# TensorE's order from block 26 to 103 of a graph layer: made block by block instead of pair by pair

## The chip, the cores and the metric

The kernel runs on one core of one Trainium2 chip. The metric is the device time of one execution in microseconds. The core's engines work from queues of their own and meet through semaphores: TensorE (PE: matrix products; PEld: its weight loads), VectorE (DVE), ScalarE (ACT), GpSimd (POOL) and SyncE (SP). Here GpSimd only issues gathers, and SP the other transfers.

## The reference, cut to what matters

One graph layer with a residual connection and a layer norm over 8192 nodes of 256 features and 131072 edges, which are sorted by their target node:

```python
ea = edge_attr @ w_e + b_e                       # [131072, 64] x [64, 256]
msg = relu(x[src] + ea)
agg = segment_sum(msg, dst, 8192)
t = x + agg
h_local = bn1(relu(t @ w1 + b1) @ w2 + b2 + x)
# attention among the 32 nodes of each group, 4 heads of 64
h_attn = bn2(attention(x) @ out_w.T + out_b + x)
out = h_local + h_attn
out = bn3(out + relu(out @ m_w1 + m_b1) @ m_w2 + m_b2)
result = layernorm(x + out)
```

## The kernel before, in words

**Edge work** goes in 128 blocks of 1024 edges. For block b:

- `gather(b)` (L152) fetches the rows x[src] with eight indirect DMAs that GpSimd issues (L157), into `xs`, a tile with four buffers. The first 20 blocks (NX) read x; the later ones read `xb`, a copy of x + b_e that the kernel itself makes in DRAM. `copy_load` (L612) loads a part of x, `copy_stream` (L617) adds b_e on VectorE (L621) and writes the part out (L623).
- `edge_products(b)` (L195) multiplies the transposed edge attributes by w_e (L208) into `pe`, two buffers of two PSUM banks. For the first 20 blocks it also adds b_e by a product (L203).
- `edge_messages(b)` (L219) adds `xs` on VectorE (L229, two halves for each block) and takes the relu on ScalarE (L233). The `xs` buffer is free after the additions.
- `next_edges(b)` (L213) transposes the edge attributes of a later block on VectorE (L190) and loads those of one two further on.
- `edge_hot(b)` (L236) builds one-hot matrices on VectorE (L241).
- `edge_sums(blocks)` (L248) sums the messages of one or two blocks by products with the one-hot matrices (L255) into the PSUM tile `pw`; ScalarE copies it to `ws` (L265), and VectorE builds a second one-hot matrix (L269).
- `edge_place(...)` (L272) puts the sums at their nodes by a product (L280) into `l2`, which shares its one PSUM bank with `pw`; VectorE adds them to the node tile `xT` (L289).

**Node work** goes in 16 chunks of 512 nodes: `attention_front` (L424: transposes, query and key products at L445), `attention_back` (L452: values at L459, scores at L476, softmax, attention at L514, output at L526) and `dense` (L535: four layers at L545, transposes at L582, layer norm, store at L598). `dense` of a chunk may start when the last block that reaches it is placed. The last two chunks are cut into five parts.

**The order.** TensorE's queue is in the order in which the code is written (`tc.manual_schedule(engines={PE})`, L700); until block 26 (NV) VectorE's and ScalarE's are too, and from then on a scheduler orders these two. The node work lies in four streams of generators. `work.run(us)` (L651) lets them emit so many microseconds, by the planner's own costs (1.7 for a step of four matrix rows of 512); what is over or under is carried on in `owed`, to 2.0 at most. A generator that yields REST or PAUSE is left out for two or one calls of `run` (L654, L664). So the number of `run` calls counts, beside their sum. PER = 5.1 us and PER_X = 4.2 us (for the first 20 blocks) are a block's share of node work.

Until TAIL = 104 the loop at L739 goes by pairs of blocks: both gathers, the first block's products and messages, the sums of the former pair, the second block's products and messages, the placing, node work in between. Below NV the shares of a pair's node work are 0.3, 0.2 and 0.5; from NV on 0.2, 0.1, 0.2 and 0.5. From TAIL on a planner (L781 to L827) orders by times: gathers arrive every 10.035 us (`came`), and the step that is due goes next. `s` and `l` are the next block to be summed and to be placed.

Of the kernel before, what the change touches and what calls it, by code (L numbers as in the profile page):

```python
# [40 lines left out]
NV = 26  # L41
TAIL = 104
# [18 lines left out]
def first_node(b):  # L61
    return b * NPB - SLACK[b]
# [10 lines left out]
def gnn_kernel(ctx: ExitStack, tc: tile.TileContext, x, src, dst, edge_attr, w, out):  # L73
# [72 lines left out]
    def bank2():  # L146
        return pps.tile([P, 2, CH], FP, name="pe", tag="pe", bufs=2)
# [4 lines left out]
    def gather(b):  # L152
        xs = epool.tile([P, NH, TJ, C], FP, name="xs", tag="xs", bufs=4)
        for h in range(NH):
            for j in range(TJ):
                idx = srcd[:, b * NH + h, j : j + 1] if b < ND else srci[:, b, h * TJ + j : h * TJ + j + 1]
                nc.gpsimd.indirect_dma_start(  # L157
                    out=xs[:, h, j, :],
                    out_offset=None,
                    in_=x if b < NX else xb[:, :],  # L160
                    in_offset=bass.IndirectOffsetOnAxis(ap=idx, axis=0),
                )
        xs_of[b] = xs
# [31 lines left out]
    def edge_products(b):  # L195

        eaT = eaT_of.pop(b).rearrange("p (h m) r -> p h (m r)", h=NH)
        for h in range(0, NH, 2):
            pe = bank2().rearrange("p i (u c) -> p i u c", u=2)
            half = [slice(i * ED, (i + 1) * ED) for i in range(2)]  # L200
            if b < NX:
                for i, rows in enumerate(half):
                    nc.tensor.matmul(  # L203
                        pe[:, i], sel[rows, :], be[rows, None, :].to_broadcast([ED, 2, C]), start=True, stop=False, skip_group_check=True
                    )
            for u in range(2):
                for i, rows in enumerate(half):
                    nc.tensor.matmul(  # L208
                        pe[:, i, u, :], eaT[rows, h + u], we[rows, :], start=(b >= NX), stop=True, skip_group_check=True
                    )  # L210
            pe_of[b, h] = pe

    def next_edges(b):  # L213
        if b < NB:
            edge_transpose(b)
        if b + 2 < NB:
            load_edges(b + 2)
# [18 lines left out]
    def edge_hot(b):  # L236

        oh = oh_of[b] = epool.tile([P, TB, WN], FP, name="oh", tag="oh", bufs=2)
        for t0 in range(0, TB, TB // 2):
            ts = slice(t0, t0 + TB // 2)  # L240
            nc.vector.tensor_tensor(  # L241
                oh[:, ts],
                iota_n[:, None, :WN].to_broadcast([P, TB // 2, WN]),
                rel[:, b, ts, None].to_broadcast([P, TB // 2, WN]),
                ALU.is_equal,
            )
# [45 lines left out]
    stated = [True]  # L292
# [336 lines left out]
    def copy_some(n=1):  # L629
        for _ in range(n):  # L630
            next(copying[0], None)
# [63 lines left out]
    work = Work(4)  # L695
    PER = 5.1
    PER_X = 4.2
    OTHER = ("vn", "qk", "oT", "pr", "o")
    placed = -1
    with tc.manual_schedule(engines={PE}):  # L700

        def last_of(c, t_z=TN):

            return max(b for b in range(NB) if first_node(b) < c * CH + t_z * P)

        def summed(c, t_z=TN):
            last = last_of(c, t_z)
            return lambda: placed >= last and chunk[c].get("done") and not xp_of and b > 2

        for c in range(NCH):  # L710
            st, before, same = chunk[c], chunk[c - 1], chunk[c - 4]
            front = attention_front(c * CH, st, npool, bank)
            if c < 2:
                next(front)
            work.add(
                FRONT,
                lambda c=c, b=before, s=same: (c < 1 or b.get("scores"))
                and (c < 4 or s.get("dense")),
                front,
            )  # L720
            work.add(BACK, lambda s=st: s.get("front"), attention_back(st, npool, bank, bank2))
            if c < NCH - 2:
                work.add(DENSE, summed(c), dense(c * CH, st, npool, bank))
        for i, c, t_a, t_z in (
            (DENSE2, NCH - 2, 0, 2), (DENSE, NCH - 2, 2, 4), (DENSE2, NCH - 1, 0, 2), (DENSE, NCH - 1, 2, 3),
            (DENSE2, NCH - 1, 3, 4),
        ):
            d = dense(c * CH, chunk[c], npool, bank, t_a, t_z, *([OTHER] if i == DENSE2 else []))
            ready = summed(c, t_z)
            if i == DENSE2:  # L730
                ready = lambda r=ready: r() and chunk[NCH - 1].get("done")
            work.add(i, ready, d)

        spots.append(copy_some)
        early = ExitStack()
        early.enter_context(tc.manual_schedule(engines={mybir.EngineType.DVE, mybir.EngineType.Activation}))
        sums, waiting = None, []
        b = 0
        while b < TAIL:  # L739
            if b == NV:  # L740
                early.close()
                stated[0] = False
            blocks, per = range(b, b + 2), 2 * (PER_X if b < NX else PER)
            copying[0] = copy_stream(b // 2 - 1)
            for i in blocks:
                if i + 2 < NB:
                    gather(i + 2)
                if 4 <= i < 8:
                    wt, name = ((w1, "w1"), (w2, "w2"), (mw1, "m_w1"), (mw2, "m_w2"))[i - 4]
                    nc.sync.dma_start(wt, w[name].rearrange("(k p) m -> p k m", p=P))  # L750

            if b:
                edge_products(b)
                edge_messages(b)
                next_edges(b + 2)
            if waiting:
                sums = edge_sums(waiting)
            waiting = list(blocks)
            if not stated[0]:
                work.run(0.2 * per)  # L760
            edge_products(b + 1)
            edge_messages(b + 1)
            next_edges(b + 3)
            if stated[0]:
                for i in blocks:
                    edge_hot(i)
                    copy_some(2)
            work.run((0.3 if stated[0] else 0.1) * per)
            copy_load(b // 2)
            if sums:  # L770
                edge_place(*sums)
                placed, sums = sums[0][-1], None
            work.run(0.2 * per)
            if not stated[0]:
                for i in blocks:
                    edge_hot(i)
            work.run(0.5 * per)
            copy_some(4 * TN)
            b += 2

        came = [7.9 + 10.035 * (i + 1) for i in range(NB)]  # L781
        t, p, m, s, l = came[b - 2] + 20, b, b, b - 2, b - 2
        added = dict((i, came[i] + 2.0) for i in range(b))
        summed_at, bank_free = {}, t
        work.at = [t] * len(work.streams)
        while l < NB:

            times = [1e9] * 4
            if l < s:
                times[0] = summed_at[l] + 1.5  # L790
            elif s < m:
                times[1] = max(added[s] + 1.2, bank_free)
            if p < NB and m == p:
                times[2] = added[p - 1]
            if m < p:
                times[3] = came[m]
            if t >= times[0]:
                edge_place(*sums)
                placed = l
                t += 0.75  # L800
                bank_free = work.placed_at = t + 0.7
                l += 1
            elif t >= times[1]:
                sums = edge_sums([s])
                t += 1.2
                summed_at[s] = t
                s += 1
            elif t >= times[2]:
                if p + 2 < NB:
                    gather(p + 2)  # L810
                edge_products(p)
                next_edges(p + 2)
                edge_hot(p)
                t += 2.1
                p += 1
            elif t >= times[3]:

                with ExitStack() as behind:
                    for i in newest.values():
                        behind.enter_context(tc.issue_after(i))  # L820
                    edge_messages(m)
                added[m] = max(t, came[m], added[m - 1] + 0.5) + 2.0
                m += 1
            elif l == s - 1 == NB - 1:
                t = times[0]
            else:
                t = work.step(t, min(times))  # L827
        work.finish()
# [124 lines left out]
```

## Time and profile before

| | |
|---|---|
| median of 3 runs (range) | 1314.89 us (1314.71 to 1315.25) |
| the profiled execution: its time, its span | 1315.3 us, 1313.3 us |
| busy: TensorE, weight loads | 1196.5 us (91%), 720.4 us (55%) |
| busy: VectorE, ScalarE, GpSimd | 800.9 (61%), 589.2 (45%), 976.1 us (74%) |
| mean granted TensorE clock | 0.959 of full |
| DMA | 240.34 MB, 183 GB/s |

The span goes from the first to the last instruction; an execution's time holds about 2 us more. In a timeline row the columns are start, duration (us), engine, line, operation, output <- inputs and how many were merged; in brackets stand the idle time of the engine just before it and what ended it. In a table of waits they are the engine and line that waited, for whom, microseconds in total, times, and the longest.

### The profile page before, as it was taken

The page shows a single profiled execution, that of the slowest core. Times are in us where ns is not written, and L with a number is a line of the kernel's source. Part 1 is how long each engine was busy: PE and PEld are TensorE (multiplying, and loading weights), DVE is VectorE, ACT ScalarE, POOL GpSimd, SP SyncE. Part 2 cuts the span into 40 slices and gives each one's busy share as a digit, 9 for nine tenths or more (in the row PEclk, how much of TensorE's full clock was granted, in tenths as well). Part 3 has the DMA queues.
Part 4 walks back from the last instruction along what each step waited for, and adds up shares of the span by engine and source line. Part 5 has one row for each costly group of instructions (what it writes and reads, how often), then busy time and mean ns, then how long its engine had stood idle before and what let it go on. Part 6 is the DMA issues. An engine that isn't in the chain of part 4 may idle for free.

```text
span 1313.3 us, 20960 instructions
## 1 busy us (share of the span) xinstructions
PE 1196.5 (91%) x7635; PEld 720.4 (55%) x7635; DVE 800.9 (61%) x1629; ACT 589.2 (45%) x841; POOL 976.1 (74%) x1032
## 2 busy tenths in 40 slices
PE   4987989999999989898997998989898999989987
PEld 3554655556555655554554554545556555555655
DVE  5567665756666565745646574565647558475754
ACT  2524443454545363544544444353454445444433
POOL 6777777777777777777777777777777777777772
PEclk8988999999999989998998998989898999999989
DMA  9999876677766665755757566576567567655742
GB/s 234 283 338 273 263 210 175 172 183 193 177 170 170 169 183 162 195 155 157 194 157 185 154 185 168 154 186 170 170 169 189 149 169 193 162 162 161 193 129 58
DMA packets 148905, 240.34 MB, mean 183 GB/s; under 512 B 27934, under 2 KB 112188, under 8 KB 148028
## 3 DMA queue, kind: packets, MB, share of 16 engines
q0 software_dynamic: 49152, 134.28, 38.0%
q1 hardware_dynamic: 98556, 104.65, 29.5%
q8 instruction: 62, 1.02, 0.3%
q14 instruction: 47, 0.39, 0.1%
q10 hardware_dynamic: 1088, 0.00, 0.0%
HBM read 222.06 MB, written 16.78 MB: 182 GB/s over the span
## 4 chain that ended last, share of the span: by engine, by line
PE 49%; POOL 20%; issue 10%; DMA 9%; DVE 7%; ACT 4%; SPq 0%; DVEq 0%; POOLq 0%; ACTq 0%
POOL xs L157 20%; PE at L545 13%; PE pe L208 10%; PE at L445 6%; DMA xs<-xb,srci 5%; PE pw L255 5%; PE at L526 3%; PE l L280 3%; PE pe L203 2%; DVE msg L229 2%; PE at L459 2%; DMA xs<-in_x_dram,srci 2%; PE at L514 1%; ACT pr L486 1%; DVE bd L506 1%
## 5 line engine op out<-in xcount | busy, mean ns | idle before, releaser
L157 POOL DMA_INDIRECT xs<-xb,srci x864 | 820.7, 950 | 263.4 <-issue 245.1
L233 ACT ACTIVATE msg<-msg 128x1024 f32<-128x1024 f32 (+1 forms) x259 | 270.0, 1046 | 402.6 <-DVE msg L229 398.6
L229 DVE TENSOR_TENSOR msg<-pe,xs 128x1024 f32<-128x1024 f32 (+1 forms) x259 | 306.5, 1205 | 196.0 <-PE pe L208 75.8
L208 PE MATMUL pe<-we,eaT 64*128 64x256 f32 x2048 | 267.8, 398 | 17.0 <-ACT pr L486 11.8
L208 PEld LDWEIGHTS pe<-we,eaT 64*128 64x128 f32 x2048 | 193.6, 192 | 121.2 <-issue 62.7
L157 POOL DMA_INDIRECT xs<-in_x_dram,srci x144 | 138.3, 961 | 43.9 <-issue 39.9
L255 PE MATMUL pw<-msg,oh 128*32 128x256 f32 x2048 | 128.8, 384 | 1.4 <-ACT msg L233 1.0
L545 PE MATMUL at<-hA,mw 128*128 128x512 f32 (+2 forms) x304 | 124.8, 538 | 3.4 <-DVE hA L555 3.4
L445 PE MATMUL at<-xT,inT 128*128 128x512 f32 x256 | 121.9, 602 | 3.2 <-ACT xT L435 3.2
L545 PE MATMUL at<-m,mw 128*128 128x512 f32 (+2 forms) x304 | 119.0, 534 | 0.1
L190 DVE STREAM_TRANSPOSE eaT<-ea 128x512 f32<-128x512 f32 x128 | 89.9, 702 | 24.7 <-PE pe L208 20.7
L255 PEld LDWEIGHTS pw<-msg,oh 128*32 128x32 f32 x2048 | 59.5, 110 | 63.3 <-issue 22.9
L280 PEld LDWEIGHTS l<-oh,ws 128*128 128x128 f32 x512 | 74.4, 196 | 28.1 <-issue 20.9
L280 PE MATMUL l<-oh,ws 128*128 128x160 f32 (+4 forms) x512 | 86.3, 309 | 2.4 <-ACT ws L265 1.6
L545 PEld LDWEIGHTS at<-hA,mw 128*128 128x128 f32 x304 | 54.1, 192 | 51.6 <-issue 40.8
L545 PEld LDWEIGHTS at<-m,mw 128*128 128x128 f32 x304 | 54.6, 192 | 48.7 <-issue 44.9
L445 PEld LDWEIGHTS at<-xT,inT 128*128 128x128 f32 x256 | 46.9, 191 | 57.5 <-issue 48.3
L448 ACT ACTIVATE qk<-at,vec 128x512 f32<-128x512 f32 x64 | 43.9, 685 | 74.9 <-PE at L445 74.8
L545 PE MATMUL at<-xT,w 128*128 128x512 f32 (+2 forms) x152 | 68.5, 588 | 7.4 <-DVE xT L289 7.4
L545 PE MATMUL at<-h,w 128*128 128x512 f32 (+2 forms) x152 | 65.0, 550 | 9.6 <-ACT oT L521 6.3
L561 ACT ACTIVATE m<-at,vec 128x512 f32<-128x512 f32 (+2 forms) x76 | 46.8, 618 | 56.5 <-PE at L545 56.2
L570 DVE SCALAR_TENSOR_TENSOR zT<-at,s,zT 128x512 f32<-128x512 f32 (+2 forms) x38 | 25.1, 662 | 72.0 <-PE at L545 72.0
(113 smaller groups left out, 1228.3 us busy)
## 6 DMA issues: line engine op xcount, KB each, us to landing
ea<-in_edge_attr_dram SPq DMA_DIRECT2D x512, 128.0 KB
xs<-xb,srci POOLq DMA_INDIRECT x864
xn<-in_x_dram SPq DMA_DIRECT2D x16, 512.0 KB
out_dram<-y SPq DMA_DIRECT2D x14, 512.0 KB
xp<-in_x_dram SPq DMA_DIRECT2D x10, 512.0 KB
xb<-xp SPq DMA_DIRECT2D x10, 512.0 KB
xp<-in_x_dram SPq DMA_DIRECT2D x3, 1024.0 KB
xb<-xp SPq DMA_DIRECT2D x3, 1024.0 KB
```

What stands on the lines that cost most here:

```text
L157: nc.gpsimd.indirect_dma_start(out=xs[:, h, j, :], out_offset=None, in_=x if b < NX else xb[:, :], in_offset=bass.IndirectOffsetOnAxis(ap= ...
L190: nc.vector.transpose(eaT, ea[:, QR:].rearrange("p (g d) -> p g d", d=ED)[:, :, :QR])
L208: nc.tensor.matmul(pe[:, i, u, :], eaT[rows, h + u], we[rows, :], start=(b >= NX), stop=True, skip_group_check=True)
L229: nc.vector.tensor_add(msg[:, hs, js].rearrange("p u i c -> p i u c"), pe[:, js, u : u + n, :], xs[:, hs, js].rearrange("p u i c -> p i u c"),
L233: nc.scalar.activation(msg[:, hs, js], msg[:, hs, js], AF.Relu)
L255: nc.tensor.matmul(pw[h * WN : (h + 1) * WN, i, :], oh[:, h * TJ + j, :], msg[:, h, j, :], start=(j == 0), stop=(j == TJ - 1), skip_group_ ...
L280: nc.tensor.matmul(l2[:, k, at : at + wn], ws[:, i, k * P : (k + 1) * P], oh2[:, i, :wn], start=(i == 0 and k == 0), stop=(i == last), ski ...
L445: nc.tensor.matmul(ps, inT[:, k, o * P : (o + 1) * P], xT[:, k, :], start=(k == 0), stop=(k == KC - 1))
L448: nc.scalar.activation(qk[:, o, :], ps, AF.Identity, bias=v_("in_b", o))
L526: nc.tensor.matmul(ps, outT[:, k, o * P : (o + 1) * P], oT[:, k, :], start=(k == 0), stop=(k == KC - 1))
L545: nc.tensor.matmul(ps, wt[:, k, o * P : (o + 1) * P], act[:, k, :], start=(k == 0), stop=(k == nk - 1))
L561: nc.scalar.activation(m1[:, o, :], layer(mw1, KC, o, hA), AF.Relu, bias=v_("m_b1", o))
```

## The change

The pair loop ends at block 26. There the two last shares of a pair become one of 0.7, so that a pair has two calls of `run` instead of three. A new loop goes through blocks 26 to 103 one by one: the gather, products, messages, the next edges, the sums of the former block, 0.3 of a block's node work, the placing, 0.2, the one-hot matrices, 0.5. The planner then starts with one block to be summed instead of two.

```diff
-        while b < TAIL:
-            if b == NV:
-                early.close()
-                stated[0] = False
+        while b < NV:
...
             waiting = list(blocks)
-            if not stated[0]:
-                work.run(0.2 * per)
             edge_products(b + 1)
             edge_messages(b + 1)
             next_edges(b + 3)
-            if stated[0]:
-                for i in blocks:
-                    edge_hot(i)
-                    copy_some(2)
-            work.run((0.3 if stated[0] else 0.1) * per)
+            for i in blocks:
+                edge_hot(i)
+                copy_some(2)
+            work.run(0.3 * per)
             copy_load(b // 2)
             if sums:
                 edge_place(*sums)
                 placed, sums = sums[0][-1], None
-            work.run(0.2 * per)
-            if not stated[0]:
-                for i in blocks:
-                    edge_hot(i)
-            work.run(0.5 * per)
+            work.run(0.7 * per)
             copy_some(4 * TN)
             b += 2

+        early.close()
+        stated[0] = False
+        for b in range(NV, TAIL):
+            gather(b + 2)
+            edge_products(b)
+            edge_messages(b)
+            next_edges(b + 2)
+            sums = edge_sums(waiting)
+            waiting = [b]
+            work.run(0.3 * PER)
+            edge_place(*sums)
+            placed = sums[0][-1]
+            work.run(0.2 * PER)
+            edge_hot(b)
+            work.run(0.5 * PER)
+        b = TAIL
...
-        t, p, m, s, l = came[b - 2] + 20, b, b, b - 2, b - 2
+        t, p, m, s, l = came[b - 2] + 20, b, b, b - 1, b - 1
```

## The prediction

> **What bounds the kernel now.** I read the row of GpSimd's gathers first, because the busy shares at the top of the page point to the wrong engine: TensorE is busy 91% of the span, GpSimd 74%.
>
> The gather line's own view, with its number of instructions, their durations and what GpSimd waited for:
>
> ```profile
> L157 POOL DMA_INDIRECT xs<-xb,srci x864: 942/948/1072, 207.4 to 1290.2; - x173
> L157 POOL DMA_INDIRECT xs<-in_x_dram,srci x144: 942/949/1147, 25.2 to 206.2; - x144
> ```
>
> GpSimd's waits:
>
> ```profile
> POOL xs L157 <- issue: 292.2, 951, 2.6
> POOL xs L157 <- DMA xs<-xb,srci: 5.8, 19, 0.3
> POOL xs L157 <- DVE msg L229: 3.7, 12, 0.3
> ```
>
> There are 144 + 864 + 16 = 1024 gathers, the first at 4.2 us, the last from 1290.2 to 1291.2. That is 1287.0 / 1024 = 1.257 us each: 0.95 us of work and a pause of 0.30 us that is there whoever released it (the third column, the longest wait, is 0.3 even where a semaphore is named). Eight gathers make a block, so a block is delivered every 10.05 us, and GpSimd never stood still for another engine. The windows say the same at any place: 37.8 to 38.0 us of gathers in each 50 us.
>
> The second reading is how far the rest runs behind. For each block I set the end of its last message addition on VectorE (L229, two rows a block) against the start of its last gather: the distance is 31.4 us at block 14, 17.3 at block 26, 4.0 to 4.2 at blocks 51, 55, 58, 65, 75 and 83, 10.7 at 102, 12.7 at 119, and 4.2 at 124 to 126. About 4 us is the least, the flight of the gather and the two additions. The rows buffer `xs` has four copies, so gather b+4 may start only when block b's messages are added. At 31.4 us this had 0.4 us left (message end 186.9, gather 18 at 187.3); from block 26 to 103 some 14 us or more are left.
>
> The third reading is the end. First TensorE's timeline around 1260:
>
> ```profile
> 1259.42 0.70 PE L280 MATMUL l<-oh,ws 128*128 128x112 f32 x4 [0.55 <-ACT ws L265]
> 1261.73 2.08 PE L208 MATMUL pe<-we,eaT 64*128 64x256 f32 x8 [1.61 <-DVE msg L229]
> 1264.42 2.08 PE L208 MATMUL pe<-we,eaT 64*128 64x256 f32 x8 [0.61 <-DVE msg L229]
> ```
>
> At 1261.73 it waits 1.61 us for additions that wait for a gather: it has caught up and works at GpSimd's pace. Then the timeline of all engines:
>
> ```profile
> 1290.23 0.95 POOL L157 DMA_INDIRECT xs<-xb,srci  x1 [0.30 <-issue]
> ...
> 1293.00 0.42 DVE L229 TENSOR_TENSOR msg<-pe,xs 128x256 f32<-128x256 f32 x1
> ...
> 1294.50 1.09 PE L255 MATMUL pw<-msg,oh 128*32 128x256 f32 x16
> ```
>
> After the last gather a fixed chain follows: last addition until 1293.4, sums 1294.5, place 1296.4, dense layers until 1307.5, normalisation and output to 1313.3: 22.1 us.
>
> So the span is 4.2 (start) + 1287.0 (gathers) + 22.1 (chain) = 1313.3 us. The profiled execution took 1315.3 us, 2.0 more than its span; the median of the three runs shown is 1314.89, 0.4 less.
>
> **The change part by part.** *No work for GpSimd.* The same 1024 gathers stand in the same order, and only their place in the trace of the other engines moves. Cost 0, as long as each finds its buffer free.
>
> *Blocks 6 to 25.* Two shares of 0.2 and 0.5 become one of 0.7, so a pair has two visits to the node streams instead of three, and a stream that rests two visits rests longer. I counted TensorE's orders of both programs and priced them by rows (512 columns: four rows 1.88 us; products 2.00; sums of two blocks 1.93; a chunk's attention products of L514 1.97). Ahead of block 14's products stand 55 us of node work instead of 65, ahead of block 26's 114 instead of 121. The work is put off, not lost. So the point with 0.4 us left gets looser: TensorE comes up to 10 us earlier, unless the other order makes it wait. The worst such wait in this trace is 6.3 us (at L514, for VectorE's transposes of line 506), less than 10. In the same stretch the last copy of x + b_e to `xb` is issued at 195.3 us and the first gather from `xb` starts at 207.4: 12 us that also get no shorter if TensorE is earlier. I take 0; bounds 0 and, if one stall of 6.3 us fell on GpSimd in full, +6.3.
>
> *Blocks 26 to 103, instructions.* TensorE has the same 3963 matrix instructions in both orders. ScalarE has 38 more evacuations of the sums: 76 of 256 columns (0.372 us) for 38 of 512 (0.569), 28.3 - 21.6 = +6.7 us, and two more table loads of 1.28 us, +2.6. VectorE has 38 more additions at L289; from the row of 96 columns (0.239) and that of 448 (0.599) an addition's fixed part is about 0.14 us, my estimate, so +5 us, and up to 38 x 0.24 = 9. Both engines hide this: in 267 to 1060 us ScalarE is busy 373 of 793 us and VectorE 474. SP and GpSimd get nothing new. Bounds: nothing, and if each of the 38 small copies stood whole before TensorE, 38 x 0.37 = 14 us of TensorE time, within what follows.
>
> *The same blocks, TensorE's waits.* In 267 to 1060 us it is busy 737.7 of 793.0 us, so 55 us are waits, 0.70 us a block. The change removes some: a block's products now follow the former block's by some 7 us of other work always, where the pair had them 4 us apart in one place and 9.5 in the other; the largest waits named there are for messages (14.2 us at L476) and for ScalarE (10.3 us at L208). It adds one: between sums and place there was 2.0 + 0.3 x 10.2 = 5.1 us of products and node work, now 0.3 x 5.1 = 1.5 us, in practice one step of 1.72 to 1.88. The place waits for ScalarE's copy, and ScalarE has ahead of it the first half of the newer block's messages (1.07), which waits for an addition (1.22). Behind a waiting place stand the node steps and the next products; for those waits VectorE. If all three follow one another, 1.22 + 1.07 + 0.37 - 1.72 = 0.94 us a block; if the copy is free, 0. The bounds on TensorE are thus -55 us (all waits gone) and +73 us (78 x 0.94). I take 0, since the products (2.0 us) run before the sums and let addition and message pass. For the end both bounds are small: a gain of 55 us only makes TensorE wait for gathers, and a loss is first paid out of the 55.
>
> At this place a rule of the Trainium skill speaks against the change (TensorE: Matmul & The Clock Gate, "HAM oscillation"): idle gaps over some 3.4 us put the clock at half, so waits cost twice. The granted clock here is 0.90 in the window 850 to 900, which has gaps of 2.65 and 2.52 us before L476 and L545, and 1.00 in 950 to 1000, which has none over 1.2: the trace agrees in kind, but the gaps are shorter than the page's. By it, one window of 3.4 us at half clock more in each pair would be 39 x 1.7 = 66 us of TensorE time, an estimate, near the 73 above.
>
> *The handing over at 104.* The later planner starts with one block's sums open instead of two, and with less node work behind it: ahead of block 104's products 521 us instead of 528, ahead of block 103's 516 instead of 521. By block 123 both stand at the same 626.5, and TensorE's last 196 matrix instructions, from just ahead of block 123's products, stand in the same order in both, and so do VectorE's last 80. About 5 us of node work, less 1 for sums, move into blocks 104 to 123. TensorE is idle 10.7 us in 1060 to 1250 and 6.2 us in 1250 to 1291, and between the products of blocks 124 and 125 there is no node work at all, where some 3.8 of 10 us are used. So 4 to 5 us come out before the last gather. Bounds: 0, and +5 if none is absorbed.
>
> **Sum**: 1315.3 + 0 + 0 + 0 + 0 = 1315.3 on the profiled execution's scale, 1315 with the runs' 0.4 us below it. Single gathers of 1.0 to 1.15 us beside the heavy early transfers and the interleaving of 1289 to 1294 may move it by 1 to 1.5 us.
>
> **Rivals.** A measurement of this kernel tells about 0.2% (2.6 us) from no change.
>
> *TensorE falls behind (slower).* The wait at the place costs so much in each block that it exceeds the idle time. It decides from 0.70 us a block on, at block 104, and for the end from (55 + 17 - 4) / 78 = 0.87 us. At 1.2 us it is 94 + 4 - 55 - 17 = +26 us, 1341. For it: place has 1.7 us of cover, and the chain can reach 0.94. Against: it would need nearly that worst chain every time, and a TensorE that is late finds its gathers landed, so the addition starts at once. Chance 0.10.
>
> *The put-off work is late at the end (slower).* 3 to 5 us of it are still there at block 126: 1318 to 1320. For it: TensorE runs without a gap from 1274 to 1291. Against: the gaps just before. Chance 0.06. *An early stall of GpSimd*, up to +6.3, 1321: 0.04; for it the 0.4 us at block 14, against it the 10 us less work.
>
> *TensorE was the bound after all (faster).* At 91% busy, even shares would recover part of its waits, and the end would move with it. For it only the busy share; against it GpSimd's row without a wait. What can be gained is in the chain after the last gather, of which TensorE and VectorE hold some 14 us; a quarter of it would be 1311.5. Chance 0.08.
>
> *It hardly does anything to the time*: that is my forecast, 0.72. Its own range is 1313.5 to 1317.
>
> **How the numbers follow.** Slower by over 0.2%: 0.10 + 0.06 + 0.04 = 0.20. Faster: 0.08. Within: 0.72. The range takes the forecast's, the late end and the early stall, 1313 to 1321, and leaves out the falling behind and the faster case, 0.18.
>
> **What would show it.** Right: 1024 gathers from 4.2 to about 1291 with no wait over 0.3 us; message lag smaller than 31 us at block 14, at least 10 us of buffer left later; TensorE's time busy unchanged but its waits moved; a chain of 22 us after the last gather. Wrong: a GpSimd row with a wait of microseconds for L229 or for `xb`; L280 waiting for L265 by more than 55 us in all; no wait for L229 at block 125's products; a last gather that ends at 1291 and a span that is still longer.

## The result, and the profile after

The changed kernel took 1322.38 us (median of 4 runs, 1320.92 to 1324.0) against 1315.07 us (1314.71 to 1315.86) of the kernel before: a ratio of 1.0055, 95% interval 1.0038 to 1.0073. It is slower, by more than the 0.2% that counts as a difference here, and outside the forecast range of 1313 to 1321. In twelve of the eighteen runs below the kernel before itself took 1946 to 2045 us, for a reason that stays open, and nothing is concluded from their ratios.

The profiled execution took 1320.92 us with a span of 1319.1 us, 5.8 us longer than the 1313.3 us before. First GpSimd's gathers, from the gather line's own view: instructions, their least, median and longest duration in ns, first and last start.

```profile
L157 POOL DMA_INDIRECT xs<-xb,srci x864: 942/946/1186, 209.0 to 1290.5; - x173
L157 POOL DMA_INDIRECT xs<-in_x_dram,srci x144: 942/946/2112, 25.5 to 207.8; - x144
```

GpSimd's waits after:

```profile
POOL xs L157 <- issue: 295.1, 961, 2.6
POOL xs L157 <- DMA xs<-xb,srci: 3.7, 12, 0.3
...
POOL xs L157 <- DVE msg L229: 3.0, 10, 0.3
```

The last gather starts at 1290.5 us (before 1290.2), and no wait named for another engine is over 0.3 us: the gathers are as before. After the last one (it ends at 1291.4) the kernel needs 27.7 us instead of 22.1. So the time is not lost by the gathers, but by an engine that comes late to the end. TensorE's timeline after shows it (start, duration, in brackets the idle time before and what ended it):

```profile
1267.92 0.70 PE L280 MATMUL l<-oh,ws 128*128 128x112 f32 x4 [0.55 <-ACT ws L265]
1270.23 2.27 PE L208 MATMUL pe<-we,eaT 64*128 64x256 f32 x16 [1.61 <-DVE msg L229]
...
1274.04 0.70 PE L280 MATMUL l<-oh,ws 128*128 128x112 f32 x4 [0.54 <-ACT ws L265]
1275.22 2.00 PE L545 MATMUL at<-xT,w 128*128 128x256 f32 x8 [0.48 <-DVE xT L289]
...
1278.23 1.56 PE L545 MATMUL at<-h,w 128*128 128x256 f32 x6 [0.58 <-ACT h L552]
1279.72 2.00 PE L208 MATMUL pe<-we,eaT 64*128 64x256 f32 x16
...
1288.77 2.00 PE L208 MATMUL pe<-we,eaT 64*128 64x256 f32 x16
```

The products of block 127 start at 1288.77 us; before they started at 1283.52. Those of block 123 were 8.5 us late (1258.1 against 1249.6), so 3.2 us were made up between the two. The wait of 1.61 us ahead of block 125's products, which the prediction took for a wait for a gather, is there after as well, though TensorE is then 8.5 us later: it is the fixed chain from a product to its addition to the next product. The other four (0.55, 0.54, 0.48, 0.58) are there before as well, within 0.02 us. Of before's gaps in this stretch only the one of 0.61 us is gone.

Where the 5.25 us (1288.77 - 1283.52) come from is read from the windows, cut at TensorE's own events: the products of block 26, 107 and 127. Block 107 is the last of the changed kernel whose message additions end within 5 us of the start of its last gather (4.2 us; about 4 is the least): there TensorE meets the gathers for the last time. Before, it does so again at blocks 123 to 126 (4.1 to 4.9 us). Columns: from and to, length, then for PE, PEld, DVE, ACT and POOL the busy time and its instructions, the granted clock, DMA share and GB/s. Before:

```profile
0.00:290.20 290.20, 254.43 (x1647) 152.95 (x1647) 184.16 (x398) 120.92 (x173) 218.12 (x234) 0.96 0.86 239
290.20:1088.93 798.73, 741.91 (x4685) 440.31 (x4684) 481.05 (x942) 372.42 (x513) 604.83 (x637) 0.96 0.65 171
1088.93:1283.52 194.59, 179.73 (x1137) 110.19 (x1136) 122.24 (x252) 85.20 (x128) 147.34 (x156) 0.97 0.62 166
1283.52:1313.30 29.78, 20.40 (x169) 16.91 (x168) 13.48 (x39) 10.64 (x27) 5.83 (x7) 0.93 0.18 53
```

The same after:

```profile
0.00:288.47 288.47, 250.87 (x1631) 150.15 (x1632) 183.76 (x397) 118.65 (x170) 217.32 (x232) 0.95 0.85 239
288.47:1088.30 799.83, 740.88 (x4677) 433.49 (x4676) 492.64 (x974) 372.50 (x546) 605.48 (x639) 0.97 0.66 172
1088.30:1288.77 200.47, 182.44 (x1165) 112.20 (x1161) 126.07 (x259) 90.14 (x139) 151.74 (x161) 0.98 0.61 163
1288.77:1319.10 30.33, 20.41 (x169) 16.95 (x168) 12.51 (x37) 9.84 (x27) 2.02 (x3) 0.97 0.11 35
```

Up to block 107 both stand level (1088.9 and 1088.3 us), the row that holds the block-by-block stretch is 1.1 us longer, and the last row is 0.6 longer. The loss is the third row: 200.5 us instead of 194.6, with 28 more matrix instructions in it. By the order of the two programs, 98.8 us of node work stand behind block 107's products before and 104.2 after. The experiments ask whether that is the work which the merged share of 0.7 put off below block 26, carried along for 80 blocks.

### The profile page after: what moved, and what is told of

It reads as the page before. It is cut to its first block, busy times and chain, and to the rows that moved or that the text cites. A ratio compares the mean times of both kernels' runs of the same rounds, so it can differ in the third digit from the quotient of the medians.

```text
span 1319.1 us, 21143 instructions
## 1 busy us (share of the span) xinstructions
PE 1194.6 (91%) x7635; PEld 712.8 (54%) x7635; DVE 815.0 (62%) x1667; ACT 591.1 (45%) x881; POOL 976.6 (74%) x1032
## 4 chain that ended last, share of the span: by engine, by line
PE 43%; POOL 20%; DVE 12%; issue 11%; DMA 8%; ACT 5%; SPq 1%; DVEq 0%; ACTq 0%; POOLq 0%
POOL xs L157 20%; PE at L545 13%; PE pe L208 9%; PE at L445 5%; PE pw L255 4%; DVE msg L229 4%; DMA xs<-xb,srci 4%; PE l L280 3%; PE at L526 3%; PE at L459 2%; DMA xs<-in_x_dram,srci 2%; ACT msg L233 2%; PE at L514 2%; DMA ea<-in_edge_attr_dram 2%; PE pe L203 1%
## 5 line engine op out<-in xcount | busy, mean ns | idle before, releaser
L208 PE MATMUL pe<-we,eaT 64*128 64x256 f32 x2048 | 264.2, 394 | 5.1 <-ACT pr L486 3.2
L255 PE MATMUL pw<-msg,oh 128*32 128x256 f32 x2048 | 137.3, 389 | 5.7 <-DVE xT L289 5.4
L280 PEld LDWEIGHTS l<-oh,ws 128*128 128x128 f32 x512 | 76.7, 192 | 80.4 <-ACT ws L265 39.7
L280 PE MATMUL l<-oh,ws 128*128 128x160 f32 (+4 forms) x512 | 90.5, 304 | 31.5 <-ACT ws L265 25.6
L255 PEld LDWEIGHTS pw<-msg,oh 128*32 128x32 f32 x2048 | 55.9, 110 | 76.2 <-issue 37.1
L289 DVE TENSOR_TENSOR xT<-l,xT 128x320 f32<-128x320 f32 (+11 forms) x145 | 57.0, 410 | 46.0 <-PE l L280 44.8
L241 DVE TENSOR_TENSOR oh<-iota_n,rel 128x128 f32<-128x128 f32 x256 | 59.4, 272 | 21.8 <-PE pw L255 21.8
```

The source lines that it names most:

```text
L208: nc.tensor.matmul(pe[:, i, u, :], eaT[rows, h + u], we[rows, :], start=(b >= NX), stop=True, skip_group_check=True)
L241: nc.vector.tensor_tensor(oh[:, ts], iota_n[:, None, :WN].to_broadcast([P, TB // 2, WN]), rel[:, b, ts, None].to_broadcast([P, TB // 2, WN ...
L255: nc.tensor.matmul(pw[h * WN : (h + 1) * WN, i, :], oh[:, h * TJ + j, :], msg[:, h, j, :], start=(j == 0), stop=(j == TJ - 1), skip_group_ ...
L280: nc.tensor.matmul(l2[:, k, at : at + wn], ws[:, i, k * P : (k + 1) * P], oh2[:, i, :wn], start=(i == 0 and k == 0), stop=(i == last), ski ...
L289: newest["xT"] = nc.vector.tensor_add(xT, l2[:, :, a - n : z - n], xT).ins
```

## The experiments

**Theory 1** is this: the work that was put off below block 26 (6.9 us by the order) is what makes the end late, since TensorE has no free time to do it later. Against it stand theory 2, that the block-by-block order itself, with its new waits, costs the time, and theory 3, that the merged call does so in another way than by the amount put off, as by the order that it gives the chunks.

### early_back: the three calls below block 26 again, block order kept

```diff
-            work.run(0.7 * per)
+            work.run(0.2 * per)
+            work.run(0.5 * per)
```

The two calls follow each other where the changed kernel has its one, so only the count of calls differs.

> The same kernel again, since in its first runs both kernels took over 2000 us, with some 40 stretches of about 14 us in which VectorE and ScalarE stood still, which the first runs of before and after do not have. The changed kernel with the three calls (0.3, 0.2, 0.5) below block 26 restored; blocks 26 to 103 block by block. Theory 1, the end is late because node work is put off below block 26: 1314 to 1316, products of block 127 at about 1283.5 us. Theory 2, the order by blocks itself makes TensorE wait more: 1320 to 1324.

Measured: 1315.46 us (12 runs), ratio to before 1.0009 (0.9996 to 1.0022), the span of the profiled execution 1313.4. The first and third rows of its windows:

```profile
0.00:288.84 288.84, 254.72 (x1647) 153.14 (x1647) 183.77 (x398) 120.78 (x173) 217.27 (x233) 0.96 0.86 240
...
1088.82:1281.85 193.03, 176.02 (x1125) 108.42 (x1125) 119.72 (x244) 86.43 (x130) 146.06 (x154) 0.99 0.63 168
```

One line brings the time back, and the third row is 193.0 us. Ahead of block 26 TensorE is busy 254.7 us instead of 250.9 and comes to its products at the same time (288.8 and 288.5): there the work was free, and where it was left out TensorE was idle 37.6 us instead of 34.1. The block order itself costs nothing that this measurement can tell: the interval leaves at most 2.9 us.

### early_only: the merged call alone, pairs kept to block 103

```diff
-            work.run(0.2 * per)
-            if not stated[0]:
+            if stated[0]:
+                work.run(0.7 * per)
+            else:
+                work.run(0.2 * per)
                 for i in blocks:
                     edge_hot(i)
-            work.run(0.5 * per)
+                work.run(0.5 * per)
```

> The same kernel again, for the same reason. The kernel before with only the calls below block 26 changed; from 26 on pair by pair. Theory 1 (work put off, 6.9 us less node work ahead of block 104's products): 1319 to 1324. Theory 2 (the order by blocks): 1314 to 1316.

Measured: 1327.29 us (6 runs), 1.0086 (1.0068 to 1.0104), span 1325.3: later, as theory 1 says, but 3 us beyond the 1324 that was expected of it. Its third and last stage:

```profile
1085.50:1291.42 205.92, 185.43 (x1163) 115.98 (x1161) 126.25 (x259) 90.24 (x139) 154.20 (x163) 0.96 0.61 162
```

```profile
1291.42:1325.30 33.88, 24.48 (x169) 20.18 (x168) 12.52 (x37) 9.93 (x27) 0.00 (x0) 0.81 0.06 18
```

The put-off work alone makes the kernel slower than the whole change does. 104.2 us of node work are left at block 107, as in the changed kernel, and the stage takes 11.3 us more than before: 5.7 us are busy time, with 5.4 us more of work, and 5.6 are idle time. One wait of 5.3 us, put down to VectorE's normalisation (L588), is not in the changed kernel. The last stage is 4.1 us longer than before, all of it TensorE's busy time (24.5 instead of 20.4) at a granted clock of 0.81.

### pair_less: the work put off in another place, all else as before

```diff
-            blocks, per = range(b, b + 2), 2 * (PER_X if b < NX else PER)
+            blocks, per = range(b, b + 2), 2 * (PER_X if b < NX else PER if b < NV else 5.0)
```

> Pair by pair, below block 26 as before, a share of 5.0 instead of 5.1 us from 26 on: 6.9 us less node work ahead of block 104's products. Theory 1 (put-off work comes out at the end, whatever put it off): 1320 to 1328. Theory 3 (the calls below block 26 do their harm in some other way): 1314 to 1316.

Measured: 1324.78 us (8 runs), 1.006 (1.0041 to 1.0079). The profiled execution, with a span of 1328.3 us, was the longest of the eight (1321.98 to 1330.12). Calls and order are those of before; a share of 5.0 us instead of 5.1 leaves the same 104.2 us at block 107:

```profile
1088.30:1294.00 205.70, 186.56 (x1164) 116.67 (x1160) 126.17 (x259) 90.46 (x139) 153.04 (x162) 0.95 0.61 161
```

Again products of 107 at 1088.3 and a stage of 205.7 us. Work that is left late in another place comes out at the end too.

### share517 and share530: the work given back from block 26 on

```diff
-            work.run(0.3 * PER)
+            work.run(0.3 * 5.17)
```

and so for the shares of 0.2 and 0.5; share530 has 5.3. By the order, 98.8 us are left at block 107 in the first, as before, and 87.9 in the second.

> The changed kernel with a share of 5.17 instead of 5.1 us from block 26 to 103; the two calls below block 26 kept. By block 104 TensorE has had the same total as before the change (-0.1 us). Theory 1 (put-off work comes out at the end): 1314 to 1317. Theory 3 (the calls below block 26 do their harm in some other way): 1320 to 1324.

> The changed kernel with a share of 5.3 us: 12.1 us more ahead of block 104's products than before the change. If from some point on only the gathers bound the end, nothing is gained over before: 1313 to 1316. If TensorE's put-off work bounds it all along, some 10 us below before: 1303 to 1308.

Measured: share517 1320.81 us (12 runs), 1.0031 (1.0013 to 1.005), span 1317.0; share530 1330.52 us (6 runs), 1.0107 (1.0082 to 1.0131), span 1326.3. Theory 1, as it was put, missed both, the second by 14 us and more, and the first lies where theory 3 had put it (1320 to 1324). The windows of share517, blocks 26 to 107 and 107 to 127:

```profile
286.51:1093.51 807.00, 742.92 (x4718) 435.02 (x4717) 495.17 (x980) 377.33 (x556) 610.88 (x644) 0.97 0.64 171
1093.51:1286.60 193.09, 176.95 (x1124) 108.52 (x1120) 123.61 (x253) 86.09 (x129) 146.18 (x155) 0.99 0.62 165
```

And of share530:

```profile
286.50:1110.80 824.30, 761.43 (x4781) 445.42 (x4780) 503.79 (x1006) 381.37 (x565) 623.88 (x658) 0.97 0.64 171
1110.80:1295.75 184.95, 165.35 (x1059) 102.03 (x1057) 113.67 (x227) 78.83 (x118) 137.30 (x145) 0.99 0.61 161
```

The last stage answers as the theory says: 193.1 us with 98.8 left, 185.0 with 87.9. But the middle stage grew: against the changed kernel's 799.8 us by 7.2 and 24.5 us, for 5.4 and 16.3 us of work moved into it. So TensorE's idle time there (59 us) is not free time: with the work added it rose to 64 and 63 us. In share530 no message addition after block 26 ends less than 9 us behind the start of its block's last gather, where about 4 is the least: TensorE never meets the gathers any more and is itself the bound. In share517 it does meet them. Its timeline just before block 107's products:

```profile
1081.52 1.16 PE L476 MATMUL pe<-qk 64*128 64x128 f32 x16 [1.77 <-DVE msg L229]
1085.89 2.08 PE L476 MATMUL pe<-qk 64*128 64x128 f32 x16 [3.21 <-DVE msg L229]
1087.89 4.68 PE L545 MATMUL at<-m,mw 128*128 128x512 f32 x8
1092.51 1.07 PE L255 MATMUL pw<-msg,oh 128*32 128x256 f32 x16
```

And on VectorE:

```profile
1084.52 1.23 DVE L229 TENSOR_TENSOR msg<-pe,xs 128x1024 f32<-128x1024 f32 x1 [3.14 <-DMA xs<-xb,srci]
```

The scores of an attention chunk (L476) use the `pe` buffers of the products, and wait 5.0 us for additions; the second of these had itself waited 3.14 us for gathered rows. Then 4.7 us of node work come before block 107's products. Being early here is worth nothing, and TensorE reaches block 107 4.6 us later than before.

### early_more62: the work given back below block 26, calls still merged

```diff
-            blocks, per = range(b, b + 2), 2 * (PER_X if b < NX else PER)
+            blocks, per = range(b, b + 2), 2 * (PER_X if b < NX else 6.2)
```

The results so far leave two causes: the amount, or the merged call by the order that it makes. Here the order of the kernels gives 122.7 us of node work ahead of block 26 (before 120.9, changed 114.1). What is called theory 2 in the expectation is here the reading of share517, that work given back late does not land.

> The changed kernel with its share per block raised from 5.1 to 6.2 us in the pairs below block 26 that follow the first stretch; the calls stay merged there, and block order and share from 26 on stay as changed. By the order of the kernels, TensorE's node work ahead of block 26's products is 122.7 us (before 120.9, changed 114.1) and ahead of block 104's 528.1 (before 528.1, changed 521.2). Theory 1 (the amount put off past block 26 is the loss, however it is put off): products of block 127 at 1281 to 1285 us, and 1314 to 1317 us. Theory 2 (work given back later does not land, because TensorE then waits at the gathers' heels, as with the share of 5.17): here it is given back below block 26, where TensorE runs 11 us and more behind the gathers, so 1314 to 1318. Rival (the merged call itself, by the order that it gives the chunks, costs the time, and the amount is only a sign of it): 1320 to 1324, as in the changed kernel.

Measured: 1316.40 us (12 runs), 1.0007 (0.999 to 1.0024). All four stages of its profiled execution, which at 1321.27 us was one of its longer ones (1315.22 to 1323.3):

```profile
0.00:300.27 300.27, 260.00 (x1652) 152.53 (x1652) 183.95 (x397) 120.32 (x173) 225.26 (x242) 0.96 0.85 234
300.27:1090.40 790.13, 734.04 (x4691) 428.88 (x4690) 492.50 (x976) 372.97 (x551) 598.48 (x630) 0.98 0.66 173
1090.40:1284.78 194.38, 177.46 (x1129) 110.02 (x1128) 121.88 (x256) 86.88 (x130) 147.17 (x156) 0.97 0.62 165
1284.78:1319.50 34.72, 24.61 (x169) 20.11 (x168) 13.63 (x39) 10.75 (x27) 6.03 (x7) 0.80 0.16 47
```

It comes to block 26 11.8 us later than the changed kernel, for 8.6 us more work, and is at block 107 only 2.1 us behind it: the stage between is 9.7 us shorter, with 2.2 us less work, 2.9 us less idle time, and the clock at half for 37.1 us instead of 44.4. It has 97.8 us left there and needs 194.4. Block 127's products start at 1284.78, within the 1281 to 1285 expected. The calls are still merged and the time is back: the amount is the cause, and theory 3 falls. That this one execution is long lies in its last row, a clock of 0.80 and 4.2 us more of TensorE's busy time than before.

### The other runs

These are the twelve named in the first section. Share517 alone lies on both sides of before there, so they tell nothing of the theories. The double dose of put-off work, share500, thus stays untried under the conditions of the result.

Early_back: 2028.36 us, ratio 0.9971 (0.9939 to 1.0002).

> The changed kernel with one thing undone: below block 26 a pair's node work is again given out in three calls (0.3, 0.2, 0.5). Blocks 26 to 103 stay block by block. Node work ahead of block 104's products: 528.1 us, as before the change (the changed kernel 521.2). Theory 1, the end is late because about 5 us of node work are put off into blocks 104 to 123, and they were put off below block 26: back to 1314 to 1316, products of block 127 at about 1283.5 us. Theory 2, the order by blocks itself makes TensorE wait more (the placing for ScalarE's copy): stays at 1320 to 1324.

Early_only: 2029.78 us, ratio 1.0014 (0.9971 to 1.0057).

> The kernel before with only the calls below block 26 changed (0.3 and 0.7 instead of 0.3, 0.2, 0.5); from block 26 on pair by pair as before. Node work ahead of block 104's products: 521.2 us instead of 528.1. Theory 1 (work put off): 1319 to 1324. Theory 2 (the order by blocks): 1314 to 1316.

Pair_less: 2030.48 us, ratio 1.0039 (1.0007 to 1.007).

> The kernel before, pair by pair, unchanged below block 26; from 26 on a block's share of node work is 5.0 instead of 5.1 us. Node work ahead of block 104's products: 521.2 us instead of 528.1, so the same amount is put off, in another place and without any order by blocks. Theory 1 (work put off): 1319 to 1324, whatever put it off. Theory 2: 1314 to 1316.

Pair_less again: 1987.07 us, ratio 1.0106 (1.007 to 1.0143).

> Pair by pair as before, below block 26 as before, but a share of 5.0 instead of 5.1 us from 26 on: 6.9 us less node work ahead of block 104's products. Theory 1 (what is put off into blocks 104 to 123 comes out at the end, whatever put it off): 1320 to 1328. Theory 3, that the calls below block 26 do their harm in some other way than by work put off: 1314 to 1316.

Pair_less again: 1982.62 us, ratio 1.0079 (1.0035 to 1.0123).

> The same kernel again; in its first two sets of runs all kernels took about 2000 us, with stretches of some 14 us in which VectorE and ScalarE stood still. Pair by pair, below block 26 as before, a share of 5.0 instead of 5.1 us from 26 on: 6.9 us less node work ahead of block 104's products. Theory 1 (put-off work comes out at the end, whatever put it off): 1320 to 1328. Theory 3 (the calls below block 26 do their harm in some other way): 1314 to 1316.

Share517: 2016.12 us, ratio 0.9928 (0.9894 to 0.9963).

> The changed kernel with a share of 5.17 instead of 5.1 us in the loop over blocks 26 to 103; below 26 as in the changed kernel. Node work ahead of block 104's products: 526.3 us, and with the one block more that is summed TensorE has the same total ahead of it as before the change (-0.1 us). Theory 1 (work put off): 1314 to 1317. Theory 2 (the order by blocks): 1320 to 1324.

Share517 again: 2017.22 us, ratio 1.0238 (1.0178 to 1.0299).

> The changed kernel, its two calls below block 26 kept, with a share of 5.17 instead of 5.1 us from block 26 to 103: by block 104 TensorE has had the same total as before the change (-0.1 us). Theory 1: 1314 to 1317. Theory 3 (harm below block 26 in some other way): 1320 to 1324.

Share517 again: 2001.93 us, ratio 1.017 (1.0122 to 1.0218).

> The same kernel again, for the same reason. The changed kernel with a share of 5.17 instead of 5.1 us from block 26 to 103: by block 104 TensorE has had the same total as before the change. Theory 1: 1314 to 1317. Theory 3: 1320 to 1324.

Share517 again: 2013.71 us, ratio 1.0271 (1.0184 to 1.0359).

> The changed kernel with a share of 5.17 instead of 5.1 us from block 26 to 103; the two calls below block 26 kept. By block 104 TensorE has had the same total as before the change (-0.1 us). Theory 1 (put-off work comes out at the end): 1314 to 1317. Theory 3 (the calls below block 26 do their harm in some other way): 1320 to 1324.

Share500, the changed kernel with a share of 5.0 from block 26 to 103: 1993.67 us, ratio 1.0159 (1.0092 to 1.0226).

> The changed kernel with a share of 5.0 instead of 5.1 us: 12.2 us less ahead of block 104's products than before the change (the changed kernel 5.3). Theory 1: later than the changed kernel by about the 6.9 us more that are put off, 1327 to 1332. Theory 3: as the changed kernel, 1320 to 1324.

Share530: 1986.39 us, ratio 1.0015 (0.9954 to 1.0076).

> The changed kernel with a share of 5.3 us: 12.1 us more ahead of block 104's products than before the change. If from some point on only the gathers bound the end, nothing is gained over before: 1313 to 1316. If TensorE's put-off work bounds it all along, some 10 us below before: 1303 to 1308.

Early_more62: 1995.81 us, ratio 1.0126 (1.0066 to 1.0186).

> This is the changed kernel with its share per block raised from 5.1 to 6.2 us in the pairs below block 26 that follow the first stretch; the calls stay merged there, and block order and share from 26 on stay as changed. By the order of the kernels, TensorE's node work ahead of block 26's products is 122.7 us (before 120.9, changed 114.1) and ahead of block 104's 528.1 (before 528.1, changed 521.2). Theory 1 (the amount put off past block 26 is the loss, however it is put off): products of block 127 at 1281 to 1285 us and 1314 to 1317 us. Theory 2 (work given back after it was put off does not land, because TensorE then waits at the gathers' heels, as with the share of 5.17): here the work is given back below block 26, where the gathers are still far ahead, so 1314 to 1318. Rival (the merged call itself, by the order that it gives the chunks, costs the time, and the amount is only a sign of it): 1320 to 1324, as in the changed kernel.

### The stages side by side

| kernel | ratio to before | products of 26 at | 26 to 107 | work left at 107 | 107 to 127 | additions of 126 behind the gather | products of 127 at | span |
|---|---|---|---|---|---|---|---|---|
| before | 1 | 290.2 | 798.7 | 98.8 | 194.6 | 4.2 | 1283.5 | 1313.3 |
| early_back | 1.0009 | 288.8 | 800.0 | 96.1 | 193.0 | 4.1 | 1281.9 | 1313.4 |
| early_more62 | 1.0007 | 300.3 | 790.1 | 97.8 | 194.4 | 4.1 | 1284.8 | 1319.5 |
| share517 | 1.0031 | 286.5 | 807.0 | 98.8 | 193.1 | 5.0 | 1286.6 | 1317.0 |
| changed | 1.0055 | 288.5 | 799.8 | 104.2 | 200.5 | 7.4 | 1288.8 | 1319.1 |
| pair_less | 1.006 | 289.4 | 798.9 | 104.2 | 205.7 | 13.5 | 1294.0 | 1328.3 |
| early_only | 1.0086 | 288.2 | 797.3 | 104.2 | 205.9 | 12.4 | 1291.4 | 1325.3 |
| share530 | 1.0107 | 286.5 | 824.3 | 87.9 | 185.0 | 12.6 | 1295.8 | 1326.3 |

Times are of single profiled executions, in us. The seventh column is the time from the start of block 126's last gather to the end of its last message addition: before and the two kernels level with it still meet the gathers there (4.1 to 4.2), the five slower ones do not (5.0 to 13.5). From the products of block 127 on, the three that are latest without a slow clock at the very end (changed, share517, share530) need 30.3 to 30.6 us, before 29.8.

## Why the prediction was wrong

**The bound: half right.** The gathers are as forecast in the kernels of the table, with no wait named for another engine over 0.3 us but one of 1.4 us in share530. But GpSimd was not the only bound. TensorE finished its work just as the gathers did, with the 0.61 us ahead of half of block 125's products as its whole reserve in the last blocks, apart from half-speed clock (below). The prediction read the wait of 1.61 us there as "it has caught up and works at GpSimd's pace". Nor does the last gather alone start the "fixed chain" of 22.1 us: the same pieces stand around the last addition in the changed kernel, which starts 5.1 us later (1298.13 against 1293.00) though the last gather starts only 0.2 us later (1290.46 against 1290.23). Before, gathers and TensorE reach that addition at about the same time, so the sum of gathers and chain came out right without showing the second path.

**Blocks 6 to 25: the mechanism right, the price misplaced.** "The work is put off, not lost" holds: the last addition of block 14 ends 18.1 us behind the start of its last gather instead of 31.4, and no stall fell on GpSimd. Taking 0 for the edit was right for its own stretch only.

**Instructions in 26 to 103: right that they are hidden.** ScalarE's busy time rose by 1.9 us in the whole run (591.1 against 589.2; +9 was forecast), VectorE's by 14.1 (815.0 against 800.9; 5 to 9 was forecast), and early_back, which has all of them, is level with before. One cost that was put at nothing was there, though: TensorE's instructions are the same in number, but the sums (L255) take 137.3 us instead of 128.8 in the whole run and the places (L280) 90.5 instead of 86.3, and as much more in early_back (136.8 and 90.3). What offset it, by its size, was the clock, at half for 82.6 us instead of 109.0 (early_back 67.0), which no step had forecast.

**TensorE's waits in 26 to 103: right.** They changed places and hardly their sum. From the products of block 26 to those of 127, TensorE's waits before (waiter, whom for; us in total, times, longest):

```profile
PE pe L476 <- DVE msg L229: 14.2, 9, 2.7
PE pe L208 <- ACT pr L486: 11.8, 8, 3.1
PE at L582 <- DVE zT L570: 7.0, 4, 2.8
...
PE at L514 <- DVE bd L506: 5.0, 2, 3.0
```

And after:

```profile
PE l L280 <- ACT ws L265: 25.6, 22, 3.3
PE at L514 <- DVE bd L506: 18.2, 4, 9.9
PE at L582 <- DVE zT L570: 13.9, 5, 4.3
PE pe L476 <- DVE msg L229: 3.9, 3, 1.8
```

The wait at the place (L280) is there, 25.6 us in 22 waits where the worst case was 0.94 us in each of 78 blocks, 73 in all. From 26 to 107 TensorE's idle time is 59.0 us after and 56.8 before. The rule of the Trainium skill that the prediction weighed here (TensorE: Matmul & The Clock Gate, "HAM oscillation"), by which more gaps would cost an estimated 66 us, did not decide: from the products of 26 to those of 127 the clock stood at half for 78.5 us before and 51.2 after, though one wait of 9.9 us is new.

**The handing over at 104: here it failed.** The step said: "TensorE is idle 10.7 us in 1060 to 1250 and 6.2 us in 1250 to 1291 … So 4 to 5 us come out before the last gather", and took 0, with +5 as the bound if none was absorbed. The amount was right (5.4 us more left at block 107). What failed is that idle time was taken for free time. Between the products of blocks 123 and 127 TensorE was idle 5.7 us before and 5.1 after: nearly all of it are the fixed waits of a chain (1.29, 0.55, 1.61, 0.54, 0.48, 0.58), which shift along with a late TensorE. Of the 3.2 us made up there, 2.6 are busy time (25.6 us against 28.2), since before had 6.8 us of half clock in that stretch and the changed kernel none, which is luck; 0.6 are idle time. Between 104 and 123 its idle time even rose, from 10.7 to 13.3 us. The bound of +5 was a little short as well: the span is 5.8 us longer, the median 7.3.

**The rivals.** "The put-off work is late at the end" (0.06, 1318 to 1320) was the mechanism, and its own symptom came true: "a last gather that ends at 1291 and a span that is still longer". Its price was too low by 2 to 4 us, and the argument against it, "the gaps just before", is the failed step again. "TensorE falls behind" did not happen by the wait at the place. Share530, though, shows that TensorE can be the bound of the whole stretch. "TensorE was the bound after all" forecast the wrong sign, but its reading of the bound was nearer than its 0.08: work that is put off on TensorE shows in the end nearly in full.

**What stays open.** Why share517 takes back only part of the loss is read from one trace (waits at the heels of the gathers, node work at the wrong side of block 107), not tried: early_more62 has waits at L476 in the same place (1.77 and 2.59 us) and is level. How early_more62 makes up its lateness between blocks 26 and 107 is also read from one trace, and the clock has a part in it. The same holds for the 8 us by which share530's middle stage grew beyond the work added. And pair_less and early_only lose 5 us more between 107 and 127 than the changed kernel with the same work left. By the windows 4.1 and 3.0 us of this are busy time, with the clock at half for 20.5 and 17.1 us there instead of 6.8, and 1.1 and 2.5 are idle time; the wait of 5.3 to 5.4 us for L588 stands in both, but wasn't taken away.

## What to carry to other kernels

Idle time of an engine counts as a reserve only where a row says that it ends when the bound engine delivers. A gap that another chain ends (product, addition, product) moves along when the engine is late, and absorbs nothing; look whether the same gap recurs at the same length. When an edit changes how often a scheduler is called, count the work ahead of several points of the order, above all the last point at which the engine still meets the bound one: what is left behind that point comes out at the end. And where work is given back counted here: below block 26 TensorE's lateness was made up before that point, from block 26 on the work came on top.

## What was not expected of the hardware

The granted clock decides several microseconds at the very end. What follows the products of block 127 holds 20.4 us of TensorE's busy time in 29.8 to 30.6 us at a clock of 0.92 to 0.97 (before, changed, share517, share530), and 24.5 to 24.6 us in 33.9 to 34.7 us at 0.80 to 0.81 (early_only, pair_less, early_more62), with the same 169 instructions: 4.1 us or more on the path that sets the end. Among the 17 runs of the kernel before beside early_more62, 14 lie between 1314.4 and 1318.0 us and three between 1320.8 and 1321.8, and those of early_more62 reach from 1315.2 to 1323.3. One profiled execution alone can thus be some 5 us off its median in this kernel.

When the clock halves can be worked out from the same traces, with TensorE's busy time as they model it. In the eight of the table all 137 half-clock stretches begin on a fixed grid of 3.41 us, and in the 3.41 us ahead of each TensorE was busy 1.93 us at most. Of the 2654 grid windows from 50 us on that were at full clock and were followed by full clock, none had less than 1.47 us. So a gap of 2.13 us (before, at 692.2 us) was followed by half clock and one of 2.83 us (at 536.3) was not: what counts is how a gap lies on the grid. Behind the products of block 127 the leanest window ahead of the last dense layers held 1.81 to 1.93 us in the three executions with the slow end, and 1.96 to 2.23 in the five others. That this parts the short and the long executions of one kernel is likely, but not shown.
